# Two images at a time through the 3x3 convolutions of a pre-activation block, by F(4,3) in both directions

## The chip, the core and the metric

The kernel runs on one core of a Trainium2 chip. A core has five engines, each with its own queue of instructions that it works off in order: TensorE (PE: matrix products from SBUF into PSUM; the loading of its weights is shown as PEld), VectorE (DVE), ScalarE (ACT), GpSimd (POOL) and SyncE (SP, which here only issues DMAs). The metric is the time of one execution on the device in microseconds (us), as the median of several runs.

## What is computed

The input is x of 8 images, 512 channels, 32x32 pixels, fp32. The result is x plus a block of convolutions with attention on the group-normed x (`cbs` is convolution, batch norm in evaluation form, then silu):

```python
def bot_attention(x, qkv_w, rw, rh):
    b, c, h, w = x.shape
    hw = h * w
    qkv = conv2d(x, qkv_w, 0).reshape(b, 3, HEADS, HD, hw)
    q, k, v = (qkv[:, 0], qkv[:, 1], qkv[:, 2])
    r = (rw + rh).reshape(1, HEADS, HD, hw)
    logits = jnp.einsum('bhdi,bhdj->bhij', q, k + r) * HD ** (-0.5)
    a = jax.nn.softmax(logits, axis=-1)
    out = jnp.einsum('bhij,bhdj->bhdi', a, v)
    return out.reshape(b, c, h, w)

t = cbs(x, cv1_w, cv1_bn, 0)              # 1x1, 512 -> 512
ys = [t[:, :C], t[:, C:]]                 # y0, y1: C = 256 channels each
for i in range(N):                        # N = 2 bottlenecks
    yi = ys[-1]
    z = cbs(yi, m_cv1_w[i], m_cv1_bn[i], 1)          # 3x3, 256 -> 256
    z = bot_attention(z, m_qkv_w[i], m_rw[i], m_rh[i])   # 4 heads of 64, 1024 positions
    z = jax.nn.silu(bn_eval(conv2d(z, m_cv2_w[i], 0), m_cv2_bn[i]))
    ys.append(yi + z)
return cbs(jnp.concatenate(ys, axis=1), cv2_w, cv2_bn, 0)   # 1x1, 1024 -> 512
```

`x` there is the group norm of the input over 32 groups; the block's result is added to the input.

## The kernel before

Channels lie on the 128 partitions, positions on the free axis; a tile of 256 channels has two parts (k = 0, 1). One image goes through all stages, then the next:

group norm and cv1 (for all but the first, computed behind the image before, in pieces placed inside its attentions) -> 3x3 convolution of bottleneck 0 -> qkv projection -> attention -> `m2` with the residual -> 3x3 convolution of bottleneck 1 -> projection -> attention -> `m2` -> cv2, silu, residual, output.

**The 3x3 convolution** (`conv3x3`, L955; its products are L972) is a Winograd convolution: F(4,3) in the row direction, so six transformed rows per four output rows, and F(2,3) in the column direction, so four transformed columns per two output columns. That is 24 products, each over 8 x 16 = 128 tiles of an image. The six rows are worked in three pairs i (`PAIRS` = 3). `tiles_in` (L391 to L447) transforms the input on DVE into three tiles `v_in` (first along rows into `w_rows`, then along columns at L442, L443 and L445). For each half oc of the output channels and each i there are 2 rows x 4 columns x 2 k x 2 column groups of 64 output channels = 32 matmuls of 64 columns. ACT copies one of four results out of PSUM (L452), DVE combines them (`columns_out`, L453 to L456) and, once the row pairs are there, `rows_out` (L458 to L483) makes z, on which ACT applies the silu.

The transformed weights u are computed once, in the first image, by `make_u` (L321) on DVE, stored to HBM, and loaded again for each image and bottleneck by `load_u` (L347) on SP's queue: six tiles of 1 MB for a convolution, into a ring of five (`ring`, L110). y0 and y1 of an image stay in SBUF until its cv2 has used them.

**The projection** (`project_strassen`, L611; p_ps and pv_ps are L630 and L634) makes q, k and v by Strassen's scheme, seven products of half matrices for eight, with the sums and differences on DVE. `first_sum` (L605), the first of these sums, is taken inside the convolution. The first projection of image 0 is plain (`project`, L564). Part of the qkv weights is held in SBUF; their sums `sq` are computed once and loaded from HBM.

**The attention** (`attention_fast`, L709) goes over 4 heads x 8 blocks j of 128 keys: logits on PE (L734), exp on ACT into a tile `pt` (L738; six buffers), running sums of the pt tiles on DVE into `acc` (L752, L754), products with v on PE (L768). Row sums, their reciprocal (L881) and the scaling (L842) follow. A dictionary `behind` says which work of other stages is placed after which head or block: parts of cv1 for the next image, of cv2, the group norm, and in image 0 the making of weights.

**cv1 and cv2**: for images 0 and 1 cv1 is direct (L386), for 2 to 7 it goes by Strassen (`strassen_cv1`, L1125; products L1142). cv2 goes by Strassen (`strassen`, L1036; products L1030) for images 0 to 6 and directly for the last; its last products run between `m2` of one image and the first convolution of the next. In the middle of an image the last part of the next image's cv1 (`rest`, L1174) runs between `m2` and the second convolution; meanwhile DVE has the residual adds of `m2` (L1004) and `tiles_in` for the second convolution.

**Order.** The order of each engine's instructions is settled when the program is built, by a list scheduler with the program's order, its dependences and estimated durations; `tc.issue_after(...)` holds an instruction behind another. At run time each engine goes through its list and waits on semaphores. Tiles of one tag share its buffers, so a tile can only be written when the one that had the buffer before has been read. ACT has a table for exp and another for silu, and a load (L375) stands in the list at each switch.

After all images a test of the softmax sums chooses between ending there and a general path, which does not run with these inputs.

Of the kernel before, what the change touches and what calls it, by code (L numbers as in the profile page):

```python
# [52 lines left out]
P = 128  # L53
# [3 lines left out]
HD = 64  # L57
# [4 lines left out]
def kernel(  # L62
# [29 lines left out]
    NT, NW = F // 4, F // 2  # L92
    PAIRS = 3
    NC = 4
# [4 lines left out]

# [6 lines left out]

    xs = [load_x(act, 0, c, NX) for c in range(NX // 2)]


    def ring(shape, name):  # L110
        return const.tile(shape, F32, tag="u", name=name, bufs=5)

    def load_w1():
        w = ring([P, NX, 2 * C], "w1")
        nc.sync.dma_start(w, cv1_w.rearrange("(k p) o -> p k o", p=P))
        return w

    w1 = ring([P, NX, 2 * C], "w1")

    def load_w1_half(i):  # L120
        ks = slice(i * NX // 2, (i + 1) * NX // 2)
        nc.sync.dma_start(w1[:, ks], cv1_w.rearrange("(k p) o -> p k o", p=P)[:, ks])


    def load_w2(n=2):
        nk = (2 + N) * NM // 2
        ws = [ring([P, nk, C2], f"w2_{i}") for i in range(n)]
        for i, w in enumerate(ws):
            nc.sync.dma_start(w, cv2_w[ts(i, nk * P), :].rearrange("(k p) o -> p k o", p=P))
        return ws  # L130

    def rows_of_raw(raw):
        rows = raw.rearrange("p (r c) o -> p r c o", c=3)
        return rows[:, 0::2], rows[:, 1]

    def load_raw(n, oc, k, tag, bufs=1):
        raw = act.tile([P, 9, P], F32, tag=tag, name="raw", bufs=bufs)
        nc.sync.dma_start(raw, m_cv1_w[n, ts(k, P), :, ts(oc, P)])
        return rows_of_raw(raw)

    def load_raws_y0(n, oc):

        raw = act.tile([P, 16, P], F32, tag="y0", name="raw", bufs=2)
        mid = act.tile([P, 3, P], F32, tag="xr", name="raw_mid", bufs=2)
        src = m_cv1_w[n, P : 2 * P, :, ts(oc, P)].rearrange("p (r c) o -> p r c o", c=3)
        both = raw[:, 9:15].rearrange("p (r c) o -> p r c o", c=3)
        nc.sync.dma_start(raw[:, 0:9], m_cv1_w[n, ts(0, P), :, ts(oc, P)])
        for r in range(2):
            nc.sync.dma_start(both[:, r], src[:, 2 * r])
        nc.sync.dma_start(mid, src[:, 1])  # L150
        return rows_of_raw(raw[:, 0:9]), (both, mid)

    raws = {(0, 0, 0): load_raw(0, 0, 0, "k")}
    load_w1_half(0)
    xs += [load_x(act, 0, c, NX) for c in range(NX // 2, NX)]


    KB, CO = (2 + N) * NM // 2, C2 // 2
    s_dram2 = [tc.dram_tile([P, 2, KB, CO], F32, name=f"s{i}") for i in range(2)]

    def load_ws():
        def block(o, i):
            return cv2_w[ts(i, KB * P), ts(o, CO)].rearrange("(k p) o -> p k o", p=P)

        pairs = (
            (block(0, 0), s_dram2[0][:, 0]), (block(0, 1), s_dram2[0][:, 1]),
            (s_dram2[1][:, 0], s_dram2[1][:, 1]), (block(1, 1),),
        )
        ws = []
        for i, pair in enumerate(pairs):  # L170
            w = ring([P, 2, KB, CO], f"ws{i}")
            for j, src in enumerate(pair):
                nc.sync.dma_start(w[:, j], src)
                ws.append(w[:, j])
        return ws

    def make_ws(w2):

        (a11, a21), (a12, a22) = ((w[:, :, :CO], w[:, :, CO:]) for w in w2)
        sums = [ring([P, 2, KB, CO], f"s{i}") for i in range(2)]  # L180
        s1, s4, s2, s3 = (w[:, j] for w in sums for j in range(2))

        def part1():
            nc.vector.tensor_tensor(s1, a21, a22, ALU.add)
            nc.vector.tensor_tensor(s2, s1, a11, ALU.subtract)
            nc.vector.tensor_tensor(s3, a11, a21, ALU.subtract)

        def part2():
            nc.vector.tensor_tensor(s4, a12, s2, ALU.subtract)
            return [nc.gpsimd.dma_start(dst, w) for w, dst in zip(sums, s_dram2)][-1]  # L190

        return (a11, s1, a12, s4, s2, s3, a22), part1, part2

    load_w1_half(1)

# [11 lines left out]
    raws[0, 0, 1] = load_raw(0, 0, 1, "v")  # L207
# [4 lines left out]
    for k in range(NM):  # L212
        raws[0, 1, k] = load_raw(0, 1, k, "qk"[k])

    qkv_sb = const.tile([P, N, NM, 3 * C], F32, name="qkv_sb")
# [4 lines left out]
    def load_bottleneck(n):  # L220
        nc.sync.dma_start(qkv_sb[:, n], m_qkv_w[n].rearrange("(k p) o -> p k o", p=P))
        nc.sync.dma_start(rw_sb[:, n], m_rw[n].rearrange("(k p) f -> p k f", p=P))
        nc.sync.dma_start(rh_sb[:, n], m_rh[n].rearrange("(k p) f -> p k f", p=P))
        nc.sync.dma_start(m2_sb[:, n], m_cv2_w[n].rearrange("(k p) o -> p k o", p=P))

    def block_qkv(n, o, i):
        return qkv_sb[:, n, i].rearrange("p (w c o) -> p c w o", w=3, c=NM)[:, o]

    sq_dram = [tc.dram_tile([P, 4, 3, P], F32, name=f"sq{n}") for n in range(N)]

    def make_sq(n, tag, bufs):
        (a11, a12), (a21, a22) = ([block_qkv(n, o, i) for i in range(2)] for o in range(2))
        parts = [act.tile([P, 2, 3, P], F32, tag=tag, name="sq_new", bufs=bufs) for _ in range(2)]
        s1, s2, s3, s4 = (t[:, j] for t in parts for j in range(2))
        nc.vector.tensor_tensor(s1, a21, a22, ALU.add)
        nc.vector.tensor_tensor(s2, s1, a11, ALU.subtract)
        nc.vector.tensor_tensor(s3, a11, a21, ALU.subtract)
        nc.vector.tensor_tensor(s4, a12, s2, ALU.subtract)  # L240
        for h, t in enumerate(parts):
            nc.gpsimd.dma_start(sq_dram[n][:, 2 * h : 2 * h + 2], t)

    def load_sq(n):
        w = ring([P, 4, 3, P], "sq")
        return w, nc.sync.dma_start(w, sq_dram[n])


    sw_dram = tc.dram_tile([P, 4, NX // 2, C], F32, name="sw")
# [9 lines left out]
    def make_sw(halves):  # L259
        (a11, a12), (a21, a22) = halves  # L260
        parts = [act.tile([P, 2, NX // 2, C], F32, tag="xr", name="sw_new", bufs=2) for _ in range(2)]
        s1, s2, s3, s4 = (t[:, j] for t in parts for j in range(2))
        nc.vector.tensor_tensor(s1, a21, a22, ALU.add)
        nc.vector.tensor_tensor(s2, s1, a11, ALU.subtract)
        nc.vector.tensor_tensor(s3, a11, a21, ALU.subtract)
        nc.vector.tensor_tensor(s4, a12, s2, ALU.subtract)
        for h, t in enumerate(parts):
            nc.gpsimd.dma_start(sw_dram[:, 2 * h : 2 * h + 2], t)

    def load_sw():  # L270
        w = ring([P, 4, NX // 2, C], "sw")
        nc.sync.dma_start(w, sw_dram)
        return w

# [17 lines left out]

    ypad = []
    for n in range(N + 1):
        yp = const.tile([P, NM, F + 2, F], F32, name=f"ypad{n}")
        nc.gpsimd.memset(yp[:, :, 0, :], 0.0)
        nc.gpsimd.memset(yp[:, :, F + 1, :], 0.0)
        ypad.append(yp)  # L300


# [8 lines left out]
        [[tc.dram_tile([P, NM, 2, NC, P], F32, name=f"u{n}{oc}{i}") for i in range(PAIRS)] for oc in range(NM)]  # L311
        for n in range(N)
    ]

    def new_u(name):
        return ring([P, NM, 2, NC, P], name)


    SLOT = (0, 1, 3, 2)

    def make_u(i, u, raw):  # L321


        rows, g1 = raw
        g0, g2 = rows[:, 0], rows[:, 1]
        stt, tt = nc.vector.scalar_tensor_tensor, nc.vector.tensor_tensor
        a, b = u[:, 0, 0:3], u[:, 1, 0:3]
        plus, minus = u[:, :, 1], u[:, :, 3]
        if i == 2:
            nc.scalar.copy(u[:, :, 0:3:2], rows[:, :, 0::2])  # L330
            tt(minus, rows[:, :, 0], rows[:, :, 2], ALU.add)
            tt(plus, minus, rows[:, :, 1], ALU.add)
            return tt(minus, minus, rows[:, :, 1], ALU.subtract)
        if i == 0:
            tt(b, g0, g2, ALU.add)
            tt(a, b, g1, ALU.add)
            tt(b, b, g1, ALU.subtract)
        else:
            stt(b, g2, 4.0, g0, ALU.mult, ALU.add)
            stt(a, g1, 2.0, b, ALU.mult, ALU.add)  # L340
            stt(b, g1, -2.0, b, ALU.mult, ALU.add)

        tt(minus, u[:, :, 0], u[:, :, 2], ALU.add)
        tt(plus, minus, plus, ALU.add)
        return stt(minus, minus, 2.0, plus, ALU.mult, ALU.subtract)

    def load_u(n, oc, i):  # L347
        u = new_u("u")
        nc.sync.dma_start(u, u_dram[n][oc][i])
        return u  # L350


# [11 lines left out]
    def stages(act, small, ps_big, ps_av, n_pt):  # L364
# [12 lines left out]
        def conv1x1(w_of, rhs_of, nk, ks=None, ps=None, ends=None, by_half=False):  # L377
# [7 lines left out]
            for k, half in sorted(order, key=lambda a: a[1]) if by_half else order:  # L385
                last_product[0] = nc.tensor.matmul(  # L386
                    ps[:, half, :], w_of(k), rhs_of(k, half), start=(k == begin), stop=(k == end)
                )
            return ps

        def tiles_in(yp):  # L391

# [1195 lines left out]
```

## Time and profile before

| what | value |
|---|---|
| runs | 2311.27, 2311.66, 2311.84 us; median 2311.66 |
| the profiled execution | 2310.66 us, of it span 2309.2 |
| granted clock of PE over the span | 0.998 |
| instructions | 42672 |
| HBM read, written | 198.54 MB, 34.60 MB; 101 GB/s over the span |
| exp of a pt tile (L738) | 512 of 1023 ns mean |
| running sum (L754) | 384 of 1222 ns mean |
| reciprocal (L881) | 16 of 3353 ns mean |
| loads of u on SP's queue | 85 of 1024 KB |
| table loads on ACT (L375) | 33 of 1283 ns mean |

Busy times are by engine and overlap one another; several engines work at once, so a share says how full an engine is, not what it adds to the end. [...] In a timeline, each line has the start in us from the span's begin, the length of a run of like instructions, the engine, the line, the operation, the tiles, the shapes and the count, and in brackets idle time before it with what ended it. Windows give the busy time of each engine in a stretch.

### The profile page before, as it was taken

To read this page: it belongs to the slowest core of one execution; us is meant where nothing else is said; L and a number is where in the kernel's file an instruction comes from. 1 tells how busy PE (TensorE), PEld (TensorE's weight loads), DVE (VectorE), ACT (ScalarE), POOL (GpSimd) and SP (SyncE) were. 2 spreads that over 40 slices of the span, in tenths; PEclk is the share of its full clock that TensorE was granted. 3 is DMA by queue.
4 is the path that set the end of the run, shared out by engine and by line. 5 is a ranking of instruction groups with operands and counts; after the bars stand their busy time and mean duration, and the time that the engine had idled before them with its cause. 6 is when DMAs were issued, how large, how long until landed. Compare 5 with 4: busy or idle time off the path is not lost.

```text
span 2309.2 us, 42672 instructions
## 1 busy us (share of the span) xinstructions
PE 2284.9 (99%) x17878; PEld 1163.0 (50%) x17878; DVE 1840.1 (80%) x2920; ACT 987.3 (43%) x1292; POOL 88.9 (4%) x308
## 2 busy tenths in 40 slices
PE   7999999999999999999999999999999999999998
PEld 4546355463554636446364553646436364463633
DVE  8888878888788878887788887788877988777774
ACT  2443524435254452544525354253542535335352
POOL 1000000000000000000000000000000000000000
PEclk9999999999999999999999999999999999999999
DMA  7422333041420415213161221603116040250201
GB/s 240 174 86 88 120 136 153 16 151 34 178 115 28 134 50 204 74 55 107 52 243 33 79 87 47 251 29 103 59 47 251 29 137 26 75 221 16 87 11 62
DMA packets 95545, 236.00 MB, mean 102 GB/s; under 512 B 28016, under 2 KB 50736, under 8 KB 81904
## 3 DMA queue, kind: packets, MB, share of 16 engines
q1 hardware_dynamic: 83600, 182.84, 23.2%
q0 software_dynamic: 11744, 50.34, 5.6%
q8 instruction: 143, 2.34, 0.4%
q14 instruction: 58, 0.48, 0.1%
HBM read 198.54 MB, written 34.60 MB: 101 GB/s over the span
## 4 chain that ended last, share of the span: by engine, by line
PE 96%; DVE 3%; ACT 0%; POOL 0%; DMA 0%; issue 0%; DVEq 0%; ACTq 0%
PE av_ps L768 19%; PE l_ps L734 19%; PE c_ps L972 14%; PE c L1030 8%; PE p_ps L630 8%; PE x_ps L1142 6%; PE c_new L1030 6%; PE m_ps L996 5%; PE ps L386 4%; PE pv_ps L634 3%; PE s_ps L786 1%; PE p_ps L634 1%; PE s_ps L804 1%; DVE acc L754 0%; PE v_ps L595 0%; DVE st L488 0%
## 5 line engine op out<-in xcount | busy, mean ns | idle before, releaser
L738 ACT ACTIVATE pt<-l_ps 128x1024 f32<-128x1024 f32 x512 | 495.0, 1023 | 410.0 <-PE l_ps L734 385.5
L754 DVE TENSOR_TENSOR acc<-acc,pt 128x1024 f32<-128x1024 f32 x384 | 469.4, 1222 | 65.6 <-ACT pt L738 40.1
L768 PE MATMUL av_ps<-pt,vT 64*64 64x512 f32 x4096 | 486.5, 591 | 0.5 <-DVE ao L776 0.5
L734 PE MATMUL l_ps<-q,kr 64*64 64x512 f32 x4096 | 486.0, 590 | 0.0
L972 PEld LDWEIGHTS c_ps<-v_in,u 128*64 128x64 f32 x5440 | 296.7, 137 | 10.6 <-DVE m_kept L1081 5.3
L972 PE MATMUL c_ps<-v_in,u 128*64 128x128 f32 x5440 | 300.2, 273 | 0.0
L768 PEld LDWEIGHTS av_ps<-pt,vT 64*64 64x64 f32 x4096 | 159.2, 133 | 269.4 <-issue 225.1
L734 PEld LDWEIGHTS l_ps<-q,kr 64*64 64x64 f32 x4096 | 160.0, 133 | 263.3 <-issue 252.2
L452 ACT COPY m<-c_ps 128x256 f32<-128x256 f32 x96 | 35.4, 368 | 210.2 <-PE c_ps L972 205.1
L1030 PE MATMUL c_new<-t_in,ws 128*128 128x512 f32 x288 | 124.6, 592 | 0.0
L996 PE MATMUL m_ps<-ao,m_sb 128*128 128x512 f32 x256 | 112.5, 592 | 0.0
L369 ACT ACTIVATE m_kept<-m_kept,bh,sh 128x512 f32<-128x512 f32 x42 | 31.9, 806 | 146.0 <-DVE m_kept L1114 86.3
L752 DVE TENSOR_TENSOR acc<-pt 128x1024 f32<-128x1024 f32 x64 | 78.0, 1219 | 18.1 <-ACT pt L738 18.1
L1030 PEld LDWEIGHTS c_new<-t_in,ws 128*128 128x128 f32 x288 | 54.7, 190 | 68.9 <-issue 66.0
L630 PE MATMUL p_ps<-t_z,sq 128*128 128x512 f32 x180 | 87.1, 593 | 0.0
L369 ACT ACTIVATE t<-m_ps,bh,sh 128x512 f32<-128x512 f32 x64 | 48.0, 775 | 83.9 <-PE m_ps L996 82.5
L996 PEld LDWEIGHTS m_ps<-ao,m_sb 128*128 128x128 f32 x256 | 48.6, 190 | 61.2 <-issue 61.2
L1004 DVE TENSOR_TENSOR ylast<-t,ypad 128x512 f32<-128x512 f32 x32 | 22.0, 692 | 63.2 <-ACT t L369 63.2
L369 ACT ACTIVATE z<-z,bh,sh 128x512 f32<-128x512 f32 x64 | 48.6, 806 | 54.6 <-DVE z L481 54.3
L445 DVE TENSOR_TENSOR v_in<-w_rows 128x512 f32<-128x512 f32 x96 | 65.6, 683 | 0.0
L1030 PE MATMUL c<-ypad,ws 128*128 128x512 f32 x144 | 63.8, 592 | 0.0
L1142 PE MATMUL x_ps<-t_x,sw 128*128 128x512 f32 x144 | 62.8, 592 | 0.0
(255 smaller groups left out, 2961.3 us busy)
## 6 DMA issues: line engine op xcount, KB each, us to landing
u<-u SPq DMA_DIRECT2D x85, 1024.0 KB
x<-in_x_dram SPq DMA_DIRECT2D x32, 512.0 KB
x_res<-in_x_dram POOLq DMA_DIRECT2D x32, 512.0 KB, 6.9
out_dram<-m_kept POOLq DMA_DIRECT2D x28, 512.0 KB, 7.3
u<-u_new POOLq DMA_DIRECT2D x12, 1024.0 KB, 5.2
w<-in_cv_w_dram SPq DMA_DIRECT2D x12, 1024.0 KB
rs<-r_dram SPq DMA_DIRECT2D x96, 128.0 KB
ws<-s SPq DMA_DIRECT2D x24, 512.0 KB
```

Source lines behind the costliest of these rows:

```text
L369: return nc.scalar.activation(dst, src, AF.Silu, scale=sh[:, k : k + 1], bias=bh[:, k : k + 1])
L386: last_product[0] = nc.tensor.matmul(ps[:, half, :], w_of(k), rhs_of(k, half), start=(k == begin), stop=(k == end))
L630: nc.tensor.matmul(ps[:, o, :], w[:, o, :], rhs, start=not onto, stop=True, skip_group_check=onto)
L634: nc.tensor.matmul(v[:, ts(j, P)], rhs[:, ts(j, P)], w[:, 2, :], start=j == 0 and not onto, stop=True, skip_group_check=True,)
L734: nc.tensor.matmul(ps[kh * HD : (kh + 1) * HD, hd, :], kr[r, c, o : o + HD], q[r, c, ts(half, HALF)], start=True, stop=True,)
L738: exp = nc.scalar.activation(pt[:, i], ps, AF.Exp, scale=SCALE)
L754: ins = nc.vector.tensor_tensor(accs[g], accs[g], pt[:, i], ALU.add)
L768: nc.tensor.matmul(avs[g][hd * HD : (hd + 1) * HD, kh, :], vT[r, j, o : o + HD], pt[r, i, hd, :], start=(j == 0), stop=(j == NJ - 1),)
L972: nc.tensor.matmul(ps[o, row, col, :], us[i][:, k, row, SLOT[col], o], vs[i][:, k, row, col, :], start=(k == 0), stop=(k == NM - 1),)
L996: nc.tensor.matmul(pss[oc][:, half, :], m2_sb[:, n, k, ts(oc, P)], ao[:, k, ts(half, HALF)], start=(k == 0), stop=(k == NM - 1),)
L1030: nc.tensor.matmul(ps[:, o, :], w[:, k, ts(o, P)], rhs[part][:, c, :], start=(k == 0 and not onto), stop=(k == KB - 1), skip_group_check=onto,
L1142: nc.tensor.matmul(ps[:, o, :], w[:, c, ts(o, P)], rhs[c], start=(c == 0 and not onto), stop=(c == 1), skip_group_check=onto,)
```

## The change

Images go in pairs a, b (`G` = 2, `NP` = 4). Each stage is done for a and then for b, but the 3x3 convolution is done once for both. It is F(4,3) in rows and columns: 36 products, each over 8 x 8 tiles of two images, so 128 columns again.

```diff
-    NT, NW = F // 4, F // 2
-    PAIRS = 3
-    NC = 4
+    NT = F // 4
+    TILES = NT * NT
+    G = 2
+    NP = B // G
+    NI = 3
+    CPS = ((0, 5), (1, 2), (3, 4))
+    SLOTS = ((0, 1), (2, 4), (3, 5))
+    RING = 10
```

**The weights** have six columns: u of one convolution is 18 units of 512 KB (9.4 MB), read from HBM once per pair into a ring of ten such units, on SP's queue. `make_u` has 6 columns in three row pairs, for each of two bottlenecks, oc and k (eight chunks in all); four before or in the first convolution, two in each attention of bottleneck 0 of the first pair.

**The input transform**, for both k at once:

```diff
+                e = act.tile([P, 2 * NT * NM, F + 2], F32, tag="acc", name="w_rows", bufs=2)
...
+                d = act.tile([P, 2 * NT * NM, F], F32, tag="acc", name="w_d", bufs=2)
+                tt(d, e[:, :, 2 : F + 2], e[:, :, 0:F], ALU.subtract)
+                quads = d.rearrange("p a (s j) -> p (a s) j", j=4)
+                v05, v12, v34 = (put(i, cp) for cp in range(3))
+                stt(
+                    v05.rearrange("p c q -> p q c"), quads[:, :, 0:2], -4.0, quads[:, :, 2:4], ALU.mult, ALU.add
+                )
+                stt(v34[:, 0], quads[:, :, 1], 2.0, quads[:, :, 2], ALU.mult, ALU.add)
+                stt(v34[:, 1], quads[:, :, 1], -2.0, quads[:, :, 2], ALU.mult, ALU.add)
...
+                ab = act.tile([P, 2, 2 * NT * NM, NT], F32, tag="h", name="w_ab", bufs=2)
+                stt(ab[:, 0], each4(2), -4.0, each4(4), ALU.mult, ALU.add)
+                stt(ab[:, 1], each4(1), -4.0, each4(3), ALU.mult, ALU.add)
+                a, b = (ab[:, j].rearrange("p a s -> p (a s)") for j in range(2))
+                tt(v12[:, 0], a, b, ALU.add)
+                last = tt(v12[:, 1], a, b, ALU.subtract)
```

**The products and the output transform**, for each oc and row pair i:

```diff
+                    for row in range(2):
+                        ps = ps_big.tile([P, 2, HALF], F32, tag="big", name="c3_ps")
...
+                        for cp in range(3):
+                            for c in range(2):
+                                to = slot(SLOTS[cp][c], SLOTS[cp][c] + 1)
+                                for k in range(NM):
+                                    rhs = vs[i, cp][:, c].rearrange(
+                                        "p g (r t k s) -> p g r t k s", r=2, t=NT, k=NM
+                                    )[:, :, row, :, k]
+                                    for h in range(2):
+                                        o = slice(h * HD, (h + 1) * HD)
+                                        nc.tensor.matmul(
+                                            to[o], us[cp][:, k, row, c, o], rhs, start=(k == 0), stop=(k == NM - 1)
+                                        )
+                        m24 = act.tile([P, 2, q], F32, tag="h", name="c3_m", bufs=2)
+                        nc.scalar.copy(m24, slot(4, 6).rearrange("p (a q) -> p a q", a=2))
+                        m13 = slot(2, 4).rearrange("p (a q) -> p a q", a=2)
+                        tt(m[:, row, 0::2], m13, m24, ALU.add)
+                        tt(m[:, row, 1::2], m13, m24, ALU.subtract)
+                        stt(
+                            e[:, row].rearrange("p a q -> p (a q)"), slot(0, 2), -6.0,
+                            m[:, row, 0:2].rearrange("p a q -> p (a q)"), ALU.mult, ALU.add,
+                        )
+                    r = act.tile([P, 2, q, 4], F32, tag="acc", name="c3_r", bufs=2)
+                    stt(r[..., 0], m[:, :, 2], -0.25, e[:, :, 0], ALU.mult, ALU.add)
+                    stt(r[..., 1], m[:, :, 3], -0.5, m[:, :, 1], ALU.mult, ALU.add)
+                    tt(r[..., 2], m[:, :, 0], m[:, :, 2], ALU.subtract)
+                    stt(r[..., 3], m[:, :, 3], -2.0, e[:, :, 1], ALU.mult, ALU.add)
+                    r0, r1 = (r[:, j].rearrange("p q x -> p (q x)") for j in range(2))
+                    if i < 2:
+                        tt(keep[:, i, 0], r0, r1, ALU.add)
+                        tt(keep[:, i, 1], r0, r1, ALU.subtract)
+                    if i == 1:
+                        stt(dst[:, 1], tiles(big_d), -0.5, tiles(d_), ALU.mult, ALU.add)
+                        mid = tt(dst[:, 2], tiles(s_), tiles(big_s), ALU.subtract)
+                        stt(big_s, big_s, -0.25, s_, ALU.mult, ALU.add)
+                        stt(big_d, big_d, -2.0, d_, ALU.mult, ALU.add)
...
+                    if i == 2:
+                        stt(dst[:, 0], tiles(r0), -6.0, tiles(big_s), ALU.mult, ALU.add)
+                        stt(dst[:, 3], tiles(r1), -6.0, tiles(big_d), ALU.mult, ALU.add)
```

**What goes through HBM.** y0 and y1 are stored by POOL's queue when cv1 has made them and loaded by SP's before cv2. The second convolution's v of image a is made behind `m2` of a, stored by POOL and loaded by SP before the convolution; b's is made behind `m2` of b:

```diff
+    def keep_y(b, y0s, y1):
+        for half in range(NH):
+            nc.gpsimd.dma_start(y0_dram[b][half], y0s[half])
+        nc.gpsimd.dma_start(y1_dram[b], inside(y1))
...
+        def store(i):
+            for cp in range(3):
+                nc.gpsimd.dma_start(v_dram[i][cp], v_new.pop((i, cp)))
...
+        vs = v_units()
+        for i in range(NI):
+            for cp in range(3):
+                nc.sync.dma_start(vs[i, cp][:, :, 0], v_dram[i][cp])
+        with tc.issue_after(last.ins):
+            s.tiles_in(Y2[1], putter(vs, 1))
+            check()
+
+
+        feed(units(1) + sqs(1, 0))
+        z = new_z()
+        t = s.conv3x3(1, vs, u_of(1), z, summed=z[:, :, 0])
```

**The order of stages in a pair**, each attention with parts of cv1 or cv2 behind it: convolution 0 of both; project a, attention a, m2 a, rest of the next pair's first cv1; project b, attention b, m2 b, rest of the next pair's second cv1; convolution 1 of both; project a, attention a; project b, m2 a, attention b, m2 b; cv2 of a's last products; cv2 of b; `tiles_in` of the next pair.

**The rest**: all projections go by Strassen and no qkv weights stay in SBUF; cv1 is direct for images 0 to 3 and by Strassen for 4 to 7; the pt tag keeps six buffers, shared with v and t tiles; the first pair's weights and group norms are laid out anew; the general path is carried over.

## The prediction

> **What bounds the kernel now.** I read the page's shares first, then its chain of waits, the windows of one steady image, and the engines' timelines at the edges of a convolution.
>
> ```profile
> PE 2284.9 (99%) x17878; PEld 1163.0 (50%) x17878; DVE 1840.1 (80%) x2920; ACT 987.3 (43%) x1292; POOL 88.9 (4%) x308
> ...
> PE 96%; DVE 3%; ACT 0%; POOL 0%; DMA 0%; issue 0%; DVEq 0%; ACTq 0%
> ...
> 882.68 20.60 PE c_new L1030 x48
> 903.28 21.11 PE c_ps L972 x384
> 1032.77 21.11 PE c_ps L972 x384
> ```
> TensorE (PE) is busy 99% of the span and is 96% of the chain that ended last. A convolution of one image is one unbroken piece: 384 matmuls of 64 columns in 21.11 us, 0.055 us each. The Strassen products of 128x512 take 20.60/48 = 0.429 us each.
>
> ```profile
> 903.20:924.30 21.10, 21.10 (x385) 20.94 (x384) 15.37 (x38) 4.78 (x9) 1.46 (x2) 1.00 0.97 375
> 942.90:1000.40 57.50, 57.50 (x546) 21.55 (x545) 52.28 (x69) 34.96 (x40) 1.20 (x3) 1.00 0.07 22
> 1018.90:1032.70 13.80, 13.80 (x34) 5.87 (x32) 12.73 (x28) 5.26 (x6) 0.53 (x6) 1.00 0.16 53
> 1032.70:1053.80 21.10, 21.10 (x385) 20.94 (x384) 17.59 (x49) 4.28 (x8) 0.18 (x2) 1.00 0.79 283
> ```
> The columns after the length are PE, weight loads, VectorE (DVE), ScalarE (ACT), GpSimd, granted clock, DMA share and GB/s. PE has no hole in a convolution, an attention, or the 13.8 us of cv2 products before the second convolution. But DVE fills 15 to 17.6 of each 21.1, 52 of 57.5 and 12.7 of 13.8: it is second everywhere by 1 to 6 us, so an edit that shortens PE and lengthens DVE in one stage turns the stage over.
>
> ```profile
> 1021.94 0.69 DVE L1004 TENSOR_TENSOR ypad<-t,ypad 128x512 f32<-128x512 f32 x1
> 1022.54 0.42 DVE L423 TENSOR_TENSOR w_rows<-w_tmp 128x256 f32<-128x256 f32 x1
> 1022.87 0.42 DVE L424 TENSOR_TENSOR w_rows<-w_tmp 128x256 f32<-128x256 f32 x1
> ...
> 1037.34 0.42 DVE L453 TENSOR_TENSOR r_mid<-c_ps,m 128x256 f32<-128x256 f32 x1
> ...
> 1056.89 0.42 DVE L481 SCALAR_TENSOR_TENSOR z<-sd,r_ends 128x256 f32<-128x256 f32 x1
> ```
> ```profile
> 1057.35 1.52 ACT L369 ACTIVATE z<-z,bh,sh 128x512 f32<-128x512 f32 x2
> 1058.88 1.28 ACT L375 ACT_TABLE_LOAD   x1
> ```
> ```profile
> 1058.24 1.05 PE L634 MATMUL pv_ps<-sq,t_z 128*128 128x128 f32 x8
> 1059.13 1.88 PE L630 MATMUL p_ps<-z,qkv_sb 128*128 128x512 f32 x4
> ```
> The timelines of DVE, ACT and PE around the second convolution. DVE lines start 0.33 us apart at 256 elements and 0.60 at 512: these pitches, not the durations 0.42 and 0.69, are what a line of adds costs; 1024 elements take 1.14, a dependent successor 0.1 more. m2's products end at 1018.87, the last residual add 3.7 later, then `tiles_in` runs to 1037.34, 4.6 into the convolution. The last L481 ends at 1057.31, the silus at 1058.87, and the product that reads their z starts at 1059.13: 0.26 us to spare.
>
> **The change, part by part.** *Products (PE, all on the path).* An image's convolution takes 384 matmuls, a pair's in two images 768; after it is 36 products x 2 k x 2 output halves x 2 column groups x 2 = 576 of the same 128 columns: 31.7 us for 42.2, so 8 convolutions of pairs save 8 x 10.55 = 84.4. Two more images take cv1 directly (56 Strassen steps of 128x512 become 64): 16 x 0.429 = +6.9. The first image's plain qkv becomes Strassen: -2.6. Sum -80.1: against the profiled run's 2310.7, of which 2309.2 is span, 2230.6 if nothing waits. The run is 1 us under the median, so the same sum serves.
>
> *DVE.* `tiles_in` per image and bottleneck: before 15.2 (1021.33 to 1037.34, less 0.8 of other work); after, three rounds of one 1024 add (or two of 512), two 512, one 1024, one 512 and six 256 = 1.14+1.20+1.14+0.60+2.00 = 6.1, x3 and 1.1 of dependences = 19.4. 16 x 4.2 = +67. Convolution output per pair: 60 of 256 (20.1) and 20 of 512 (12.0) with 1 to 2 of dependences = 33.5, against 2 x 14.7: 8 x 4.1 = +33. `make_u`: 9.2 per chunk against 5.8, 8 chunks: +27. So in a pair's convolution DVE needs 33.5 where PE needs 31.7, which before was 14.7 against 21.1. [...]
>
> *What waits, in a steady pair,* from the order in which the built program puts the instructions. Unstalled, the product that reads image a's finished z comes 5.3 after the 31.7, at +37.0 from the convolution's start; with 33.5 to 34.7 of DVE work and 1.1 of silu ahead of it, DVE may begin by +2.
> (1) First convolution: the tail of cv2's sums and of `tiles_in` holds DVE until +5.7; it ends at +40.4, z at +41.6: 4.6.
> (2) Project b of bottleneck 0: DVE does 12.4 of `tiles_in` and 7.3 of cv1's sums ahead of the sum that the second product group needs, while PE has 13.8 + 1.9: 4.0, and 0.5 for a late k at attention b.
> (3) Second convolution: m2 b's adds end 3.7 after its products, 18.8 of `tiles_in` follow, cv1's rest covers 13.8 (the step that the timeline above shows: 4.6 late before): DVE begins at +8.7, ends at +42.6, z at +43.8: 6.8.
> (4) Project b of bottleneck 1 follows attention a at once: two silus of cv1 and two table loads (1.28 each) stand on ACT before the copy that frees PSUM: 1.8.
> (5) Attention b of bottleneck 1: m2 a's silus, then a load for exp, before the first exp: 2.6. Behind the waiting exp stand acc's adds and av's products.
> Small ones 1. Sum 21.3, two pairs 42.6. If DVE caught up in all of (1) to (3) it were 5.4.
>
> [...] The row shows 1.28 from 1058.88 and the next ACT instruction 0.02 after it.
>
> *First pair.* PE starts at 12 as before, does two direct cv1 (2 x 27.5 plus the 2.8 that the first image loses now) and reaches the convolution at 70, needing z at 107. DVE has, from 4.6: statistics of two images 11.6, four chunks of `make_u` 36.8, two `tiles_in` 37, and waits: its first output is at 100 by the order, the last at 134.5, z at 135.7: 28.7. Each attention of bottleneck 0 carries two more chunks, 18.4: 46.3 of its own + 9.7 + 1.9 + 18.4 = 76.3 against 57.5, less 6.8 that six pt buffers allow (6 x 1.14): 11.9 each. With (3), (4), (5) 63.7, less the 6.0 of holes that image 0 has already: 57.7. Bounds: without make_u's share hidden 64, with all attention slack used 34.
>
> *Last pair.* No cv1 of a next pair covers (2): the sums, reciprocal and `tiles_in` precede the second group, 8 (0 to 13). With (1), (3), (5): 22.0.
>
> *Transfers.* A pair's convolution reads 9.4 MB of u where two images read 12; POOL stores y0, y1 and v of image a, SP loads v (2.4 MB) and, later, y. They are queued in order on SP behind a ring of ten 0.5 MB slots. 13.4 MB with qkv's weights at 375 GB/s (the window's rate) is 35.7 us, under the 38.5 that the stalled convolution has; 5 MB are there at its start. I cost it at nothing; without that lead and at the 283 GB/s of the other window it is 47, 9 more per convolution. POOL had 88.9 us of work, so its stores have room.
>
> *The moving operand* of a product is now 16 runs of 8 columns, not one of 128. No row has such runs: from 0 to a doubling of 31.7. The nearest are 128-column products in one run; I take 0.
>
> Sum: 2230.6 + 57.7 + 42.6 + 22.0 = **2353**, slower by 1.8%.
>
> **Rivals.** *A: DVE keeps up.* If after the first pair DVE begins each convolution by +2, which takes (1), (2), (3) away, what stays is 57.7 - 6.8 + 2 x 5.4 + 2.6 = 64: 2295, faster. For it: PE's 150 us of a steady image hold only 123 of DVE (the windows above are of that stretch), so there is idle DVE time; against it, none of it lies in the 13.8 before the convolution, where 12.7 are used. All waits together must stay under 80 for faster.
> *B: the ring starves PE.* Place: second convolution, where v's loads precede u on SP. 9 per convolution: 2353 + 72 = 2425. For it, a DMA share of 0.97 in the window of today; against, u is read once for two images.
> *C: short runs slow the products.* A doubling gives 8 x 31.7 = +254; it would hide (1) and (3), 46: 2560. Nothing in the profile speaks for it but the absence of such rows.
> *D: half the waits.* First pair 34, steady pairs 11 each, last 14: 2230.6 + 70 to 85 = 2301 to 2316, near no change.
>
> **How the numbers follow.** Forecast 0.58, A 0.17, D 0.10, B 0.11, C 0.04. About 0.2% (4.6 us) is what a measurement of this kernel can tell from no change. Faster is A and a third of D, 0.20; same is the middle of D, 0.05; slower the rest, 0.75. The likeliest case's own range is 2320 to 2390 (first pair 34 to 64, each steady pair -6 to +8, last 14 to 27). The range for 8 in 10 leaves out C, most of B and the lower half of A: 2292 to 2415.
>
> **What would show it.** PE's own sum falls by 80 and the holes add 120. A pair's convolution is 576 matmuls in 31.7 us. DVE's first output line lies at +5 to +9 in steady convolutions, the hole before z's product is 4 to 7 us with silu of z as its releaser, and DVE has no idle time from m2 b to there. The first pair's z product is near 136, with holes over 10 in both its attentions, released by DVE. I am wrong if holes are released by DMA (B), if the 576 take over 33 us without holes (C), or if the first output lines lie within +2 (A).

## The result, and the profile after

The changed kernel takes 2466.93 us (2465.28 to 2471.05, 4 runs) against 2311.75 (2311.27 to 2312.18) for the kernel before: a ratio of 1.067, 95% interval 1.0656 to 1.0692. The forecast was 2353, in a range of 2292 to 2415. The sign was right, the loss of 155 us is nearly four times the forecast one. The profiled execution took 2468.4, its span is 2467.0.

From the page of the kernel after: the shares, and the chain of waits.

```profile
PE 2261.3 (92%) x16378; PEld 1107.8 (45%) x16378; DVE 1991.3 (81%) x2942; ACT 1013.0 (41%) x1345; POOL 177.1 (7%) x405
...
PE 56%; DVE 21%; issue 16%; ACT 3%; DMA 2%; POOL 1%; SPq 0%; DVEq 0%; POOLq 0%; ACTq 0%
```

TensorE stood idle for 24 us of the span before and for 206 after; the chain, 96% TensorE before, runs 21% through DVE, and 16% of it ("issue") is time for which the profile shows no wait. And TensorE's busy time fell by 23.6, not by the 80.1 of the products that went: at the rates of before it would be 2204.8, so in 56.5 us of it TensorE ran slower than before. What TensorE waited for, with the total, the times and the longest:

```profile
PE c_ps L520 <- DVE c_e L528: 42.7, 15, 5.8
PE l_ps L801 <- ACT pt L805: 25.8, 12, 5.7
PE p_ps L697 <- DVE c_e L528: 19.6, 8, 2.6
PE c_ps L520 <- DVE v_in L469: 18.3, 2, 13.1
PE p_ps L697 <- ACT z L397: 14.0, 8, 1.8
PE av_ps L835 <- DVE z L843: 11.3, 4, 6.2
PE gm_ps L570 <- POOL gmat L313: 11.0, 1, 11.0
```

The first, third and fifth are the convolutions; the second and sixth are attentions, of the first pair by their times; no line of TensorE's waits is a transfer. One second convolution of a steady pair, as TensorE's timeline shows it, and under it DVE's lines at both ends of its output:

```profile
1010.91 8.08 PE L520 MATMUL c_ps<-v_in,u 128*64 128x128 f32 x144
1023.91 12.80 PE L520 MATMUL c_ps<-v_in,u 128*64 128x128 f32 x192 [4.92 <-DVE c_e L528]
1037.68 13.32 PE L520 MATMUL c_ps<-v_in,u 128*64 128x128 f32 x240 [0.97 <-DVE c_e L528]
...
1056.15 1.96 PE L697 MATMUL p_ps<-t_z,sq 128*128 128x512 f32 x4 [2.34 <-DVE c_e L528]
...
1060.81 1.98 PE L697 MATMUL p_ps<-z,sq 128*128 128x512 f32 x4 [1.81 <-ACT z L397]
```
```profile
1000.16 1.23 DVE L442 SCALAR_TENSOR_TENSOR w_ba<-ypad 128x1024 f32<-128x1024 f32 x1
...
1021.44 0.42 DVE L526 TENSOR_TENSOR c_t<-c_ps,c_m 128x256 f32<-128x256 f32 x1
...
1058.62 0.69 DVE L550 SCALAR_TENSOR_TENSOR z<-c_r,c_k 128x512 f32<-128x512 f32 x1
```

There are 576 matmuls, 240 of them in 13.32 us: 0.0555 each, the rate of before. DVE starts `tiles_in` at 1000.16 and its first output line 10.5 us after the convolution's start; from there it works with one hole of 1.2 us until 1059.9, and the product that reads z starts at +49.9, where TensorE alone would have been there at +37.0.

Where the time was lost, by pairs. The starts of the pairs' first convolutions (90.18, 743.56, 1326.55, 1910.30, end 2467.0) are set against those of images 0, 2, 4 and 6 of before (42.35, 620.50, 1186.06, 1751.62, end 2309.2), and the product time that went is added back: 21.1 per pair, with the cv1 products that lie on another side of a boundary taken into account (27.5 for one image directly, 24.0 by Strassen).

| stretch | loss forecast | loss found |
|---|---|---|
| to the second pair's convolution | 57.7 | 123.1 + 21.1 + 2.6 - 27.5 - 3.4 = 115.9 |
| second pair | 21.3 | 17.4 + 21.1 = 38.5 |
| third pair | 21.3 | 18.2 + 21.1 = 39.3 |
| last pair | 22.0 | -0.9 + 21.1 + 24.0 = 44.2 |
| sum | 122.3 | 237.9 |

237.9 less 80.1 is the 157.8 between the two spans. What is found holds TensorE's slow stretches as well as its waits.

### The profile page after: what moved, and what is told of

It reads as the page before. It is cut to its first block, busy times and chain, and to the rows that moved or that the text cites. A ratio compares the mean times of both kernels' runs of the same rounds, so it can differ in the third digit from the quotient of the medians.

```text
span 2467.0 us, 40820 instructions
## 1 busy us (share of the span) xinstructions
PE 2261.3 (92%) x16378; PEld 1107.8 (45%) x16378; DVE 1991.3 (81%) x2942; ACT 1013.0 (41%) x1345; POOL 177.1 (7%) x405
## 4 chain that ended last, share of the span: by engine, by line
PE 56%; DVE 21%; issue 16%; ACT 3%; DMA 2%; POOL 1%; SPq 0%; DVEq 0%; POOLq 0%; ACTq 0%
PE av_ps L835 14%; PE l_ps L801 13%; PE c L1047 8%; PE c_new L1047 4%; PE p_ps L697 4%; PE m_ps L1027 4%; PE ps L416 3%; PE pv_ps L701 1%; PE c_ps L520 1%; DVE acc L821 1%; PE x_ps L1153 1%; DVE w_d L466 1%; DVE v_in L469 1%; PE s_ps L852 1%; DVE c_t L526 1%
## 5 line engine op out<-in xcount | busy, mean ns | idle before, releaser
L835 PE MATMUL av_ps<-pt,vT 64*64 64x512 f32 x4096 | 492.5, 597 | 16.0 <-DVE z L843 11.3
L520 PE MATMUL c_ps<-v_in,u 128*64 128x128 f32 x4320 | 254.4, 282 | 38.8 <-DVE c_e L528 38.2
L520 PEld LDWEIGHTS c_ps<-v_in,u 128*64 128x64 f32 x4320 | 249.1, 143 | 47.6 <-ACT c_m L524 41.9
L697 PE MATMUL p_ps<-t_z,sq 128*128 128x512 f32 x256 | 130.1, 628 | 27.5 <-DVE c_e L528 19.6
L1027 PE MATMUL m_ps<-z,m_sb 128*128 128x512 f32 x256 | 113.6, 595 | 0.2
L697 PE MATMUL p_ps<-z,sq 128*128 128x512 f32 x192 | 92.2, 604 | 15.3 <-ACT z L397 14.0
L1027 PEld LDWEIGHTS m_ps<-z,m_sb 128*128 128x128 f32 x256 | 47.8, 190 | 61.7 <-issue 55.0
L697 PEld LDWEIGHTS p_ps<-t_z,sq 128*128 128x128 f32 x256 | 45.8, 200 | 62.7 <-issue 56.1
L701 PEld LDWEIGHTS pv_ps<-sq,z 128*128 128x128 f32 x384 | 51.3, 197 | 33.8 <-issue 18.4
L701 PE MATMUL pv_ps<-sq,z 128*128 128x128 f32 x384 | 53.4, 284 | 10.4 <-DVE z L843 7.7
L466 DVE TENSOR_TENSOR w_d<-w_rows 128x1024 f32<-128x1024 f32 x48 | 58.6, 1222 | 3.7 <-POOL w_rows L452 1.3
L416 PE MATMUL ps<-x,w 128*128 128x512 f32 x128 | 56.1, 594 | 0.0
```

The lines of the kernel that those rows point to most:

```text
L416: last_product[0] = nc.tensor.matmul(ps[:, half, :], w_of(k), rhs_of(k, half), start=(k == begin), stop=(k == end))
L466: tt(d, e[:, :, 2 : F + 2], e[:, :, 0:F], ALU.subtract)
L520: nc.tensor.matmul(to[o], us[cp][:, k, row, c, o], rhs, start=(k == 0), stop=(k == NM - 1))
L697: nc.tensor.matmul(ps[:, o, :], w[:, o, :], rhs, start=not onto, stop=True, skip_group_check=onto)
L701: nc.tensor.matmul(v[:, ts(j, P)], rhs[:, ts(j, P)], w[:, 2, :], start=j == 0 and not onto, stop=True, skip_group_check=True,)
L835: nc.tensor.matmul(avs[g][hd * HD : (hd + 1) * HD, kh, :], vT[r, j, o : o + HD], pt[i][r, hd, :], start=(j == 0), stop=(j == NJ - 1),)
```

## The experiments

Two explanations stood against each other. D: DVE's work sets each of these stretches, and there was more of it, and later, than the forecast had. C: TensorE's clock. The granted clock does fall. Windows of 2 us of a convolution of the first pair, behind a hole of 5.79 us that ends at 442.26 (after the length come PE, weight loads, DVE, ACT, POOL, granted clock, DMA share, GB/s):

```profile
438.00:440.00 2.00, 0.00 (x0) 0.00 (x0) 2.00 (x5) 0.00 (x0) 0.00 (x0) 1.00 0.97 365
440.00:442.00 2.00, 0.00 (x0) 0.00 (x0) 1.85 (x6) 0.74 (x2) 0.00 (x0) 0.79 1.06 442
442.00:444.00 2.00, 1.74 (x17) 1.77 (x19) 2.00 (x6) 0.00 (x0) 0.00 (x0) 0.50 0.52 217
...
446.00:448.00 2.00, 2.00 (x22) 2.00 (x20) 0.48 (x2) 0.27 (x1) 0.00 (x0) 0.50 0.92 262
448.00:450.00 2.00, 2.00 (x41) 2.00 (x39) 1.86 (x6) 0.10 (x1) 0.00 (x0) 1.00 0.62 229
```

Between 3.5 and 5.5 us into the hole, which begins at 436.47, the clock falls to 0.50, and it stays there for the first 5.7 us of work: 22 matmuls in 2 us instead of 41. Neither time is the same behind the hole of 4.92 us in the timeline above: there windows of 1 and 2 us show the clock at 0.50 from 2 to 3 us into the hole until some 4.3 us after its end. The forecast had no such term.

**No steps of 16 bytes (e1_runs).** DVE's groups of the kernel after show one size in two prices (busy, mean ns):

```profile
L527 DVE TENSOR_TENSOR c_t<-c_ps,c_m 128x256 f32<-128x256 f32 x96 | 40.1, 418 | 0.0
L469 DVE SCALAR_TENSOR_TENSOR v_in<-w_d 128x512 f32<-128x512 f32 x36 | 38.5, 1069 | 3.8 <-PE c L1047 3.8
L536 DVE SCALAR_TENSOR_TENSOR c_r<-c_t,c_e 128x256 f32<-128x256 f32 x48 | 30.5, 636 | 0.0
L480 DVE SCALAR_TENSOR_TENSOR w_ab<-w_rows 128x256 f32<-128x256 f32 x48 | 29.9, 624 | 0.0
L472 DVE SCALAR_TENSOR_TENSOR v_in<-w_d 128x256 f32<-128x256 f32 x36 | 21.7, 604 | 0.0
```

418 ns for 256 elements in a row, 604 to 640 where the instruction writes (L533 to L536) or reads (L472, L473, L479, L480) every fourth element: the four columns of a tile of F(4,3). F(2,3) before had steps of two, at 414 to 425 (L442, L443, L453 to L456 there).

```diff
-                quads = d.rearrange("p a (s j) -> p (a s) j", j=4)
+                quads = d.rearrange("p a s -> p (a s)").rearrange("p (j q) -> p q j", j=4)
...
-                    return e[:, :, m : m + F - 3 : 4]
+                    return e[:, :, m * 6 : m * 6 + NT]
...
-                    r = act.tile([P, 2, q, 4], F32, tag="acc", name="c3_r", bufs=2)
+                    r = act.tile([P, 2, 4, q], F32, tag="acc", name="c3_r", bufs=2).rearrange("p j x q -> p j q x")
...
```

> The kernel after, but the four columns of a tile are neither taken apart nor put together: tiles_in reads runs, and the convolution's r is written in runs (values land in other places; z is scaled down; the test of the sums is left out). The same instructions of the same sizes, none with a step of 16 bytes. Theory D (DVE sets the length of a convolution, and 16-byte steps made its instructions dearer than the rows of before: 0.61 us for 0.41 at 256, 1.08 for 0.69 at 512): 24 x 0.12 = 2.9 less in each output, 3.2 less in each tiles_in, so z is 5 to 6 us earlier in each of 8 convolutions and the first pair gains some more: 2467 falls by 45 to 60. Theory C (the loss over the forecast is TensorE at half clock after holes): holes over 3 us at the start of a convolution stay, so 10 to 20 at most.

2408.22 (2405.59 to 2411.11): 58.7 faster. The same groups there:

```profile
L536 DVE SCALAR_TENSOR_TENSOR c_r<-c_t,c_e 128x256 f32<-128x256 f32 x48 | 20.1, 419 | 0.0
...
L480 DVE SCALAR_TENSOR_TENSOR w_ab<-w_rows 128x256 f32<-128x256 f32 x48 | 19.8, 413 | 0.0
...
L472 DVE SCALAR_TENSOR_TENSOR v_in<-w_d 128x256 f32<-128x256 f32 x36 | 14.7, 407 | 0.0
```

Prices and time fall as D says: in the second pair z's product comes at +42.5 and +45.0 in the two convolutions, where the kernel after has +48.3 and +49.9. L469 takes 1091 ns, no less than in the kernel after (1069); its output still lies in steps. The 58.7 are half of the 115.6 us of waits that the forecast lacked (237.9 - 122.3).

**TensorE kept busy in its hole (e2_again).**

```diff
-                                for k in range(NM):
+                                again = groups == G and oc == 0 and 2 * i + row < 3 and 2 * cp + c < 3
+                                for k in [*range(NM)] * (2 if again else 1):
```

> The kernel after, with three of the six products of the first three units of each convolution done twice (same place, same result): 9 x 0.44 = 4.0 us of TensorE work put where it would stand idle for 3.8 to 5.8 us. Theory C: the clock stays up, the 1.7 to 2.9 us that the next 192 matmuls lose come back, 13 to 25 us faster although TensorE does 32 us more. Theory D: DVE sets the end of a convolution whatever TensorE does in its hole: within 5 us of the kernel after.

2470.12 (2468.09 to 2470.81), 3.2 slower than the kernel after. The hole at the start shrank to 0.66 us, the next 192 matmuls ran in 10.82 us instead of 12.80, and z's product still came at +50.6 instead of +49.9; a hole of 2.5 opened further on. With the hole filled TensorE kept its rate, 216, 192 and 240 matmuls in 12.01, 10.82 and 13.32 us, or 0.056 us each (the granted clock is 0.97 from 1008.9 to 1061, against 0.93 in the kernel after from 1010.9 to 1061), and the end did not move: in the convolutions DVE sets the end, and a slow TensorE behind a hole costs nothing on top.

**The weights of bottleneck 1 not transformed (e3_raw_u)**: `make_u` stores raw weights when n is 1.

```diff
+        if n == 1:
+            for i in (2, 0, 1):
+                for cp in range(3):
+                    u = area[:, cp * P : (cp + 4) * P].rearrange("p (r c o) -> p r c o", r=2, c=2)
+                    last = nc.gpsimd.dma_start(u_dram[n][oc][i][cp][:, k], u)
+                yield last
+            return
```

> The kernel after without the transform of bottleneck 1's weights (raw weights are stored in their place; z scaled down; the test of the sums left out): 36.8 us of DVE work less in the two attentions of bottleneck 0 of the first pair. Theory D: the holes there (14 us in the first, 16 in the second, with slow TensorE after them) go, 30 to 45 us faster. Rival (those holes come from ACT, POOL's queue or the DMAs of the first pair): less than 12.

2421.30 (2418.66 to 2426.60): 45.6 faster. Windows from z's product of the first pair to its second convolution, of the kernel after and then of this one:

```profile
160.00:428.40 268.40, 232.19 (x1410) 95.08 (x1410) 212.51 (x332) 111.79 (x155) 32.39 (x66) 0.93 0.31 109
```
```profile
159.50:382.40 222.90, 219.26 (x1408) 93.38 (x1408) 175.85 (x239) 104.92 (x131) 13.01 (x30) 1.00 0.25 83
```

With 36.7 us less of DVE's busy time the stretch is 45.5 shorter: 32.6 of it are holes of TensorE (268.40 - 232.19 against 222.90 - 219.26), and 12.9 are TensorE's busy time for the same products, at a clock of 0.93 and then 1.00. In the attentions, unlike the convolutions, the slow clock seems to be paid; that its 12.9 would come back with the clock alone was not tried.

The run doesn't part D from its rival, though: the edit takes ACT's part of `make_u` (a scaled copy and a copy in each step, 6.9 us of ACT in these windows) and 19.4 us of GpSimd's work away with DVE's. The timeline of the kernel after shows how these engines hang together at one of the holes:

```profile
193.95 0.42 ACT L363 ACTIVATE u_new<-ypad 128x256 f32<-128x256 f32 x1 [8.89 <-DVE ypad L351]
...
194.57 1.93 ACT L805 ACTIVATE pt<-l_ps 128x1024 f32<-128x1024 f32 x2
...
195.64 1.98 PE L801 MATMUL l_ps<-q,kr 64*64 64x512 f32 x8 [5.72 <-ACT pt L805]
```

ACT stood 8.89 us at a copy of `make_u` (L363) that needs DVE's L351; the exps stood behind that copy in ACT's order, and TensorE behind the exps. The holes of 4.90 (218.23) and 5.74 us (331.74) follow waits of 8.01 and 8.92 us at the same copy; over the two attentions it waited 35.3 us for DVE and 12.3 for stores of u. So DVE's work is late there, and ACT's order hands the lateness on to the exps. How much of the 45.6 is DVE's amount and how much is that order was not tried.

**No transform of b ahead of the second convolution (e4_no_b_tiles).**

```diff
                 nc.sync.dma_start(vs[i, cp][:, :, 0], v_dram[i][cp])
+                nc.sync.dma_start(vs[i, cp][:, :, 1], v_dram[i][cp])
         with tc.issue_after(last.ins):
-            s.tiles_in(Y2[1], putter(vs, 1))
             check()
```

> The kernel after without tiles_in for image b ahead of each second convolution; b's places are loaded with a's transformed input instead (the test of the sums left out). 22 us of DVE work less between m2 b and the convolution. Theory D with lateness: DVE starts the output with the first product, z's product comes 38 to 40 us after the start of the convolution and not 49.9; 4 x 10 to 12: 40 to 48 us faster. Rival (it is the pace of the output, PSUM's three buffers or ACT's copies, and not the late start): z's product stays past +45, less than 20 faster.

2442.59 (2434.19 to 2444.77): 24.3 faster, between the two. TensorE and DVE around a second convolution:

```profile
998.23 18.56 PE L520 MATMUL c_ps<-v_in,u 128*64 128x128 f32 x336
...
1036.45 3.55 PE L697 MATMUL p_ps<-t_z,sq 128*128 128x512 f32 x4 [2.55 <-DVE c_e L528]
1042.31 1.98 PE L697 MATMUL p_ps<-z,sq 128*128 128x512 f32 x4 [1.41 <-ACT z L397]
```
```profile
1001.57 0.42 DVE L526 TENSOR_TENSOR c_t<-c_ps,c_m 128x256 f32<-128x256 f32 x1 [13.61 <-ACT c_m L524]
```

DVE had nothing to do for 13.61 us before, and began at +3.3, when the first results were there (48 matmuls and ACT's copy). Still z's product came at +44.1. So there is a floor at these prices: 3.3 and 40.8 of output and silu, 7.1 more than TensorE's 37.0, however early DVE is free; the lateness is worth 5.8 more, and four times that is 23.2 of the 24.3 that this run gained. The 40.8 hold two small waits: DVE's of 1.4 us for ACT's second copy (at 1004.19), and 1.2 us in which the finished z waited behind two other copies on ACT (L730, L731) for its silus. The floor in the first convolutions was not measured by itself.

**DVE's work given to GpSimd (e5_pool_v12, e6_pool_keep, e7_pool_u)**, which had 177 us of work in 2467: one branch of `tiles_in`; three of the output's sums; the plain sums of `make_u` for bottleneck 1.

```diff
-                stt(ab[:, 0], each4(2), -4.0, each4(4), ALU.mult, ALU.add)
...
+                pool.tensor_scalar(ab[:, 0], each4(2), -4.0, None, ALU.mult)
+                pool.tensor_tensor(ab[:, 0], ab[:, 0], each4(4), ALU.add)
...
-                tt(v12[:, 0], a, b, ALU.add)
...
+                pool.tensor_tensor(v12[:, 0], a, b, ALU.add)
```
```diff
-                        tt(keep[:, i, 0], r0, r1, ALU.add)
...
+                        nc.gpsimd.tensor_tensor(keep[:, i, 0], r0, r1, ALU.add)
```
```diff
+        add = nc.gpsimd.tensor_tensor if n == 1 else tt
...
-            tt(u2, c0, c2, ALU.add)
...
+            add(u2, c0, c2, ALU.add)
```

> The kernel after, with one branch of tiles_in (two of the six columns, L479 to L483) on GpSimd as six instructions of 256 in place of four on DVE: 5.2 us of 22 off DVE in each of 16 transforms. Theory D: DVE starts the output of each convolution some 5 us earlier, never before +3.3; z earlier by 3 to 5 in 7 convolutions, and more in the first pair: 30 to 50 faster. Rival P (GpSimd's instructions are so slow, or hold DVE up so much, that v is ready no earlier): no faster, or slower.

> The kernel after, with 14 of the 80 output instructions of each convolution (L535, L539, L540) on GpSimd: 7.5 of 38 us off DVE. Theory D with the floor (DVE can't start before +3.3 and its 38 us set z's place even when it does): z 5 to 7 earlier in 8 convolutions, 40 to 56 faster. Theory of the forecast (lateness alone): nothing but the same 40, as DVE's work after its start is what it is; with rival P less than 10 or slower, since DVE then waits for GpSimd's sums.

> The kernel after, with the plain sums of the weights' transform of bottleneck 1 (9 of 256 and 3 of 384 in each of 4 chunks) on GpSimd: 17.6 us off DVE in the two attentions of bottleneck 0 of the first pair. The run without this transform at all was 45.6 faster; theory D gives 15 to 25. Rival P: less than 8, as the chain of a chunk, half on each engine, gets longer.

2537.73, 2495.28 and 2473.26 (2467.85 to 2476.14): 70.8 and 28.4 slower, and the last 6.3 slower, with runs that overlap those of the kernel after. GpSimd's groups and one of DVE's in the first of them:

```profile
L480 POOL TENSOR_SCALAR w_ab<-w_rows 128x256 f32<-128x256 f32 x48 | 84.5, 1760 | 147.1 <-DVE w_rows L458 81.4 <-issue 22.9 <-ACT t L397 18.1
...
L481 POOL TENSOR_TENSOR w_ab<-w_ab,w_rows 128x256 f32<-128x256 f32 x48 | 51.5, 1073 | 3.8
```
```profile
L472 DVE SCALAR_TENSOR_TENSOR v_in<-w_d 128x256 f32<-128x256 f32 x36 | 38.5, 1069 | 0.0
```

1.07 to 1.76 us for what DVE does in 0.41 to 0.62; and DVE's own L472, unchanged, takes 1069 ns instead of 604 beside it. Rival P holds: GpSimd is no relief, so these runs don't bear on the floor.

**Together (e9_three, e10_raw_u_all, e11_no_keep).** The first is e1, e3 and e4 at once. The second leaves out two chunks of bottleneck 0's weights too, ahead of the first convolution. The third is the first without 4.8 us of each output:

```diff
+            nc.gpsimd.memset(keep, 0.01)
...
-                    if i < 2:
-                        tt(keep[:, i, 0], r0, r1, ALU.add)
-                        tt(keep[:, i, 1], r0, r1, ALU.subtract)
```

> The three edits that helped, together: no 16-byte steps, no transform of bottleneck 1's weights, no tiles_in for b ahead of the second convolution (b's places loaded with a's; z scaled down; the test of the sums left out). Alone they gave 58.7, 45.6 and 24.3. Theory D (they shorten one chain of DVE work, at different places): nearly their sum, less 9 for the steps that lie in the left-out transforms: 2467 - 120 = 2347, from 2335 to 2360. Rival (each uncovers the next limit: TensorE's clock, DMAs): less than 90 in all, over 2377.

> Like the run without the transform of bottleneck 1's weights (2421.3), and without that of the second output half of bottleneck 0 as well: two more chunks, 18.4 us of DVE work ahead of the first convolution (z scaled down; the test of the sums left out). Theory D: DVE's first output line, at 118.6, moves to about 100, and the time falls by 14 to 20 more, to 2401 to 2407. Rival (the loads, the second group norm and ACT set the start): less than 8.

> Like the three together, and without L539 and L540, 8 of the 80 output instructions of a convolution, 4.8 us (keep holds a constant; two of four output rows get no values of their own). Theory of the floor (once DVE starts in time, its output of some 35 us from +3.3 still ends behind TensorE's 37): 2 to 4 us less in each of 8 convolutions, 16 to 32 faster than the three together. Rival (with the lateness gone TensorE, ACT's copies or PSUM's buffers set the pace): within 6 of it.

The three together: 2351.88 (2347.77 to 2354.01), 115.1 faster, near the sum that D gives. TensorE's busy time is 2230.5 there, 30.8 less than in the kernel after for the same products. The second: 2409.68 (2408.55 to 2413.13), 11.6 less than e3, between the 14 to 20 of D and the rival's 8. DVE's first output line came at 106.7, where e3 has 118.3 and the forecast of this run had 100: something besides those chunks holds the start. The third: 2334.43 (2331.56 to 2336.09), 17.4 less than the three together: with the lateness gone DVE's output still sets the pace. In the second convolution of the second pair z's product comes at +40.1 in the three together, and here at +36.9, with all 576 matmuls in one unbroken piece of 31.66 us: the +37.0 of TensorE alone.

**The chunks spread (e12_spread).**

```diff
-            behind[0] = lambda: next(chunks)
-            behind[0, 2] = lambda: next(chunks)
+            for key in ((0, 1), (0, 3), (1, 1), (1, 3), (2, 1), (2, 3)):
+                behind[key] = lambda: next(chunks)
...
-            for key in ((0, 1), (0, 2), (0, 3), (1, 1)):
+            for key in ((0, 1), (0, 3), (1, 1), (1, 3), (2, 1), (2, 3)):
```

> The kernel after, with the twelve steps of the weights' transform that lie in the two attentions of bottleneck 0 of the first pair (3.1 us of DVE each) set evenly behind the blocks of heads 0, 1 and 2, not in bunches at the start. The run without them was 45.6 faster, more than the 36.8 us of DVE work that they hold. Theory B (in a bunch they overrun the lead that six pt buffers give, each hole of 3 to 6 us is followed by TensorE at half clock): spread, the holes shrink under 3 us, the clock stays, 10 to 25 faster. Theory W (it is the amount: 76 us of DVE against 57.5 of TensorE, wherever it lies): within 8 of the kernel after.

2459.65 (2457.17 to 2461.70): 7.3 faster. Holes of 6.1 and 5.6 us stayed, one in each attention, so the place of the steps is worth little. That fits theory W, the amount; but both holes again follow waits of ACT, 7.2 and 7.4 us, at the copy L363, and no run put that copy behind the exps.

No version that computes the whole came under the kernel before; the best, this last one, takes 1.063 (1.0616 to 1.0652) of its time.

## Why the prediction was wrong

*Products, right in count and rate.* 576 matmuls at 0.0555 us each, with operands in runs of 8 columns: rival C, whose doubling was the author's estimate, fell. But the sign "PE's own sum falls by 80" did not come: it fell by 23.6, since the forecast put nothing for TensorE running slower behind holes, and that came to 56.5 us of busy time. In the convolutions it hid behind DVE (e2); in the first pair's attentions 12.9 us of it lay in the time that e3 won back.

*Transfers, right.* Not one wait of TensorE ends on a DMA: rival B fell. Queues did cost something that the forecast had not looked at: GpSimd's second instruction for `gmat` stood behind a store of u that waited for ACT, and TensorE's first matmul came at 10.95 instead of 7.69.

*DVE's prices, the first step that failed.* "`tiles_in` per image ... 19.4" and "convolution output per pair ... 33.5" took the pitch of runs for instructions that step over four elements. `tiles_in` of b took 1000.16 to 1022.44, 22 us. Output and silu took 40.8 in e4 where the forecast had 34.6; of these 6.2 the steps are about 2.9 (24 x 0.12), the two small waits 2.6, and `first_sum` (L681), which the forecast left out of the count, 0.6. Taking the steps away gave 58.7, half of the 115.6 that were missed. The traces show the price: at 256 elements 0.60 to 0.64 us in steps of four, 0.42 in runs, and 0.41 to 0.43 in the steps of two of before. What makes the step of four dear was not shown. The forecast compared only the sizes of instructions with rows of before, and no row that it used had that step.

*"DVE may begin by +2", the second.* (1) and (3) were reckoned as lateness against +2, 4.6 and 6.8, and were 11.3 (743.56 to the z product at 791.86) and 12.9. DVE's first output line came at +9.4 and +10.5, not at +5.7 and +8.7, and from there to z's product it took 39.0 and 39.4, not 35.9 and 35.1. Of (3)'s 12.9, e4 shows 5.8 to be lateness; 7.1 stay when DVE is free, since it can't begin before +3.3 and its output is longer than TensorE's products. So +2 was out of reach, and would not have been enough. This comes back eight times and is most of what the steady pairs and the last pair lost. The sign "the hole before z's product is 4 to 7 us" missed too: that hole is 1.8, and TensorE loses more of the time before, where its PSUM tiles wait for DVE's L528 (4.92, 0.97 and 2.34).

*The small waits of a steady pair.* (2) 4.5 forecast, 6.1 found; (4) 1.8, found 3.5 and released by DVE's z (L843), not by ACT's table loads; (5) 2.6, found 1.6. The places were right for (2) and (5).

*The first pair, the third.* Its convolution started at 90.2, not 70: 20 us, of which e10 shows that DVE's chunks are only a part: with two of the four gone it started at 83.5. Two waits on ACT and GpSimd (11.0 for gmat, 5.8 for the second image's norm) and 5.25 for v stand in the trace; how the 20 divide among them stays open. From there to z it took 70.0 where 65.7 were forecast. The attentions carried two chunks each for 45.5 in all, not 23.8: the holes alone were 32.6, and the slow clock behind them (12.9) was not in the sum. The step "less 6.8 that six pt buffers allow" supposes that the exps run on while DVE is late; before three of the four largest holes they stood behind ACT's copies of `make_u`, which wait for DVE, and the forecast counted `make_u` on DVE alone.

*The last pair.* 22.0 against 44.2: its two convolutions, 11.8 and 12.5, took twice their share; project b, forecast at 8, had holes of 8.8.

*The rivals.* A wanted DVE to begin by +2 and to be done in time; e4 and e9 took away the work ahead of it, and z's product still came at +44.1 and +40.1. Only e11, which leaves out 4.8 us of output as well, reaches +36.9. D, half the waits, missed the other way.

## What to carry to other kernels

A transform that gives TensorE fewer products hands VectorE more, and per stage the longer of the two counts: here 31.7 us of products stood against some 37 of output (38.6 in e4 from the first line to the last, less a wait of 1.4 and 0.6 of another sum). Price an elementwise instruction by its access step as well as its size: a wider tile turned steps of two into steps of four here, 414 to 425 ns for 256 elements into 604 to 640. And where the output of a stage is longer than its products, an earlier start moves the end only down to the first result plus that output (3.3 and 40.8 in e4, against TensorE's 37.0). Work spread over two engines also ties their orders together: here a copy on ACT that waits for late sums on DVE (8.89 us at 193.95 in the kernel after) stands ahead of exps that don't need it.

## What was not expected of the hardware

In e5, with elementwise work on GpSimd, VectorE's instructions took longer than in the kernel after: L472 1069 ns for 604, `w_d` (L466) 1449 for 1222. In the kernel after, the clock took 5.7 us of work at 0.50 to come back after a hole of 5.8, and some 4.3 after one of 4.92. Holes of 2.3 to 2.6 us ahead of the products of `t_z` left the next matmuls at their usual rate in six convolutions of eight (1.96 us for four of 128x512 at 1056.15), and slow in the first pair's two (3.24 at 153.92, 3.42 at 474.95). Adding 4 us of matmuls to each convolution, 32 in all, cost 3.2 (e2).
